# A two-layer convolution network on Trainium2: the gate's sigmoid issued at the end of the pass before its use

## The chip, the cores and the metric

The kernel runs on one NeuronCore of one Trainium2 chip. The metric is the device time of one execution in microseconds. The time before is the median of three runs.

## What is computed

The network has two layers on an input x of 8 images with 128 channels of 128 by 128, all in float32. The change touches the first layer alone. Cut to what matters, and without the batch-norm constants, that layer is:

```python
feat = gelu(bn(conv2d(x, conv_w, dilation=3)))        # 128 -> 64 channels
F2   = fft2(feat)
# attention branch: 8 heads of 8 channels
q    = F2 / l2norm(F2);  attn = complex_softmax(q @ conj(q).T * tau)
out_f = abs(ifft2(attn @ F2))
# gate branch
cg   = gelu(bn(conv1x1(F2.real)))                     # 64 -> 4 channels
cg   = sigmoid(conv1x1(cg))                           # 4 -> 64 channels
gate = abs(ifft2(cg * F2))
y    = concatenate([out_f, gate], 1) + x
```

The second layer is a 3 by 3 convolution, a Mamba scan over 8 tokens per pixel, a group norm and a silu, with a residual. It takes the first layer's result.

## The kernel before

The first layer (`layer0`) takes the images two at a time, so it has four rounds, p = 0 to 3. Each round has two parts that follow one another: `convolve(p)`, which is almost all matmul, and `spectral(p)`, in which the change lies. The order of instructions on every engine is the order in which the Python code issues them (`tc.manual_schedule` over all engines); no planner moves anything. The FFTs are matmuls against cosine and sine matrices.

`spectral(p)` is a loop of 33 passes, n = 0 to 32. Pass n works on four of the 2 x 64 channels (NP = 32 groups, the last turn only ends the last group). In the order of issue, a pass in the middle of the loop is:

- `columns(n)`: the column transforms er and ei of group n on TensorE (L293, L295), from the tile fa.
- `gate_begin(n + 2)`: four Identity activations on ScalarE (L315) that start the gate's sum cg for the group two passes ahead. They need the tile hid, which is ready early in the stage.
- `gated(n)`: four multiplies on VectorE (L335 to L338) of er and ei by the gate cg of group n, into gp.
- `rows(n + 1)`: the row transform ps of the next group on TensorE (L284) and its copy to fa on ScalarE (L286).
- `rows_back(n - 1)`: the last transform ops of the group before (L354), its Abs on ScalarE (L356), the sum with the residual on VectorE (L357, into og) and the store of og (L358) from the SP queue.
- `gate_end(n + 2)`: three multiply-add pairs on GpSimd (L325, L328; on VectorE for the first two groups), and then the sigmoid on ScalarE (L329). The sigmoid waits for the last add.
- from pass 3 on `mixture()`, which has nothing to do with the gate: it is the attention branch of four rows of the image. It has two matmuls into the tile pf (L384, L385; pf has one buffer), two squares on ScalarE (L387, L388) and a sum into feat on VectorE (L389), which frees pf. In passes 1 and 2 the softmax of the attention is done in its place, and in pass 1 this has an Exp on ScalarE (L424).
- `columns_back(n)`: eight pairs of matmuls into zps (L345, L346), and the copy to z on VectorE (L348). The next pass's ops needs z.
- in an even pass a second `mixture()`.
- `roots()`: each time that 16 rows have been mixed, a Sqrt on ScalarE over 16 rows (L399), a sum with the residual on GpSimd (L400), two stores of feat (L402), and two loads of the next residual rows (L374), all these DMAs from the SP queue.
- `load_gate(n + 3)`: a load of residual rows into xg (L365), which waits for a sum L357.

There are 32 row blocks to mix, one in an odd pass and two in an even one from pass 4 on, so they are used up in pass 24, and `roots()` does its work at the end of passes 5, 8, 10, 13, 16, 18, 21 and 24. Below these are called root passes. Passes 25 to 31 have no mixture. In an odd pass VectorE sums feat (L389) ahead of copying z (L348).

Engines execute their instructions in the order of issue, so ScalarE's queue in a pass is: L315 four times, L286, L356, L329, then L387 and L388 once or twice, and in a root pass L399. Sigmoid and Sqrt each need their own function table (ACT_TABLE_LOAD); there are 44 such loads at L329, 11 in each round.

Of the kernel before, what the change touches and what calls it, by code (L numbers as in the profile page):

```python
# [141 lines left out]
def layer0(ctx, tc, x, w0, c0, x1):  # L142
# [19 lines left out]
    def cf(name):  # L162
        at, n = C0[name]
        return ct[:, at:at + n]
# [36 lines left out]
    NP = 2 * CD // 4  # L201
# [64 lines left out]
    def spectral(p):  # L266

        with tc.tile_pool(name="l0_f1", bufs=1) as f1, \
# [11 lines left out]
            def rows(key, src, j0):  # L280

                ps = p1.tile([P, 4, P], F32, name="ps")
                for k in range(4):
                    nc.tensor.matmul(ps[:, k], src[:, :, j0 + k], cf("fwd"), start=True, stop=True)  # L284
                fas[key] = f2.tile([P, 4, P], F32, name="fa")
                nc.scalar.copy(fas[key], ps)  # L286

            def columns(key, which):

                a, out = fas.pop(key), []  # L290
                for name, of_re, of_im in (("er", "cos", "sin"), ("ei", "nsin", "cos"))[:which]:
                    e = p1.tile([P, 4, NF], F32, name=name)
                    nc.tensor.matmul(  # L293
                        e, cf(of_re), a[:, :, 0:NF], start=True, stop=False, skip_group_check=True)
                    nc.tensor.matmul(  # L295
                        e[:, :, mid], cf(of_im), a[:, :, NF:P], start=False, stop=True,
                        skip_group_check=True)
                    out.append(e)
                return out

            def hidden(b):
                er, = columns(("m", b), 1)
                for m in range(MID):
                    nc.scalar.activation(
                        hid[:, b, m, :], er[:, m, :], AF.Gelu, bias=gt[:, m:m + 1], scale=gs[:, m:m + 1])

            def place(n):
                return n * 4 // CD, n * 4 % CD

            def gate_begin(n):  # L310
                b, c = place(n)
                cgs[n] = f3.tile([P, 4, NF], F32, name="cg")
                for i in range(4):
                    k = (c + i) * MID
                    nc.scalar.activation(  # L315
                        cgs[n][:, i, :], hid[:, b, 0, :], AF.Identity, bias=b2[:, c + i:c + i + 1],
                        scale=w2[:, k:k + 1])

            def gate_end(n):

                b, c = place(n)
                eng = nc.vector if n < 2 else nc.gpsimd
                for m in range(1, MID):
                    t = f2.tile([P, 4, NF], F32, name="cgt")
                    eng.tensor_mul(  # L325
                        t, hid[:, b, m:m + 1, :].broadcast_to([P, 4, NF]),
                        w2r[:, c:c + 4, m:m + 1].broadcast_to([P, 4, NF]))
                    eng.tensor_add(cgs[n], cgs[n], t)  # L328
                nc.scalar.activation(cgs[n], cgs[n], AF.Sigmoid)  # L329

            def gated(n, e):
                er, ei = e
                cg = cgs.pop(n)
                gp = f1.tile([P, 2, 4, P], F32, name="gp")
                nc.vector.tensor_mul(gp[:, 0, :, 0:NF], er, cg)  # L335
                nc.vector.tensor_mul(gp[:, 1, :, NF:P], er[:, :, mid], cg[:, :, mid])
                nc.vector.tensor_mul(gp[:, 1, :, 0:NF], ei, cg)
                nc.vector.scalar_tensor_tensor(  # L338
                    gp[:, 0, :, NF:P], ei[:, :, mid], -1.0, cg[:, :, mid], ALU.mult, ALU.mult)
                return gp  # L340

            def columns_back(n, gp):
                zps = p1.tile([P, 4, P], F32, name="zps")
                for i in range(4):
                    nc.tensor.matmul(zps[:, i, :], gp[:, 0, i, :], cf("cos"), start=True, stop=False)  # L345
                    nc.tensor.matmul(zps[:, i, :], gp[:, 1, i, :], cf("nsin"), start=False, stop=True)  # L346
                zs[n] = f2.tile([P, 4, P], F32, name="z")
                nc.vector.tensor_copy(zs[n], zps)  # L348

            def rows_back(n):  # L350
                (b, c), z = place(n), zs.pop(n)
                ops = p1.tile([P, 4, W], F32, name="ops")
                for i in range(4):
                    nc.tensor.matmul(ops[:, i, :], z[:, i, :], cf("inv"), start=True, stop=True)  # L354
                og, xg = f2.tile([P, 4, W], F32, name="og"), xgs.pop(n)
                nc.scalar.activation(ops, ops, AF.Abs)  # L356
                nc.vector.tensor_add(og, ops, xg)  # L357
                nc.sync.dma_start(  # L358
                    x1[2 * p + b][CD + c:CD + c + 4, :, :].rearrange("c h w -> h c w"), og)

            def load_gate(n):
                if n < NP:
                    b, c = place(n)
                    xgs[n] = f3.tile([P, 4, W], F32, name="xg")
                    nc.sync.dma_start(  # L365
                        xgs[n], x[2 * p + b, CD + c:CD + c + 4, :, :].rearrange("c h w -> h c w"))
# [4 lines left out]
            def load_mixture(r0):  # L371
                mix[r0] = f2.tile([P, CH, W], F32, name="xr")
                for b in range(2):
                    nc.sync.dma_start(  # L374
                        mix[r0][b * CD:(b + 1) * CD], x[2 * p + b, 0:CD, r0:r0 + CH, :])
# [31 lines left out]
            def softmax(k):  # L407
                if k == 0:
                    nc.vector.tensor_copy(gm, gram)
                    nc.vector.tensor_mul(dg, gm, cf("ident"))  # L410
                    nc.vector.tensor_reduce(rn, dg, AX.X, ALU.add)
                    nc.vector.tensor_scalar(rn, rn, float(HW), NRM_EPS, ALU.mult, ALU.add)
                    nc.scalar.activation(rn, rn, AF.Sqrt)
                    nc.vector.reciprocal(rn, rn)
                    nc.vector.tensor_scalar(gm, gm, rn, None, ALU.mult)
                elif k == 1:
                    t = p1.tile([P, 2, 4, W], F32, name="pf")
                    nc.tensor.transpose(t[:, 0, 0, :], gm, cf("ident"))
                    nc.vector.tensor_scalar(gm, t[:, 0, 0, :], rn, tau_hw, ALU.mult, ALU.mult)
                    nc.vector.tensor_mul(gm, gm, cf("mask"))  # L420
                    nc.vector.tensor_add(gm, gm, cf("nmask"))
                    nc.vector.tensor_reduce(mx, gm, AX.X, ALU.max)
                    nc.vector.tensor_scalar(gm, gm, mx, None, ALU.subtract)
                    nc.scalar.activation(gm, gm, AF.Exp)  # L424
                elif k == 2:
                    nc.vector.tensor_reduce(rn, gm, AX.X, ALU.add)
                    nc.vector.reciprocal(rn, rn)
                    nc.vector.tensor_scalar(gm, gm, rn, None, ALU.mult)
                    t = p1.tile([P, 2, 4, W], F32, name="pf")
                    nc.tensor.transpose(t[:, 0, 0, :], gm, cf("ident"))  # L430
                    nc.vector.tensor_copy(pT, t[:, 0, 0, :])
# [7 lines left out]
            rows(0, fT, 0)  # L439
            hidden(1)  # L440
            gate_end(0)
            softmax(0)
            load_mixture(H - CH)
            load_mixture(H - 2 * CH)
            gate_begin(1)
            gate_end(1)
            for n in range(NP + 1):
                if n < NP:
                    e = columns(n, 2)
                    if n + 2 < NP:  # L450
                        gate_begin(n + 2)
                    gp = gated(n, e)
                    if n + 1 < NP:
                        b, c = place(n + 1)
                        rows(n + 1, fT, b * CD + c)
                if n > 0:
                    rows_back(n - 1)
                if n == NP:
                    break
                if n + 2 < NP:  # L460
                    gate_end(n + 2)
                if n >= START:
                    mixture()
                elif n > 0:
                    softmax(n)
                columns_back(n, gp)
                if n >= START and n % 2 == 0:
                    mixture()
                roots()
                load_gate(n + 3)  # L470
                if n == NP - 5 and 2 * p + 2 < B:
                    first_load(p + 1)
# [603 lines left out]
```

## Time and profile before

| what | value |
|---|---|
| runs, median (lowest to highest) | 15495.08 us (15492.82 to 15495.69) |
| profiled execution, its own time | 15497.77 us |
| span of the profiled execution, first to last instruction | 15495.1 us |
| mean granted TensorE clock | 0.983 |
| spectral stage of round 0, from the last Gram matmul | 333.3 us to about 662 us |
| the same of rounds 1, 2, 3 | from 988.4, 1643.7, 2299.1 us |
| second layer begins | about 2632 us |
| first ei matmul to last ei matmul of a spectral stage | 314.4, 314.7, 314.7, 314.7 us |

The profile has the start and duration of every instruction on each engine, in microseconds from the start of the span. A bracket after an instruction gives the time that its engine had been idle before it, and whose work ended that idle time. A view of waits adds such idle times up: total, number, longest. PE is TensorE's matmuls, PEld its weight loads, DVE is VectorE, ACT is ScalarE, POOL is GpSimd and SP the queue that issues DMAs. The durations of matmul groups overlap a little, since matmuls are pipelined.

A pass's length is taken here from the start of its first ei matmul to that of the next pass. In the fourth spectral stage the lengths in us are, with R for a root pass:

```
 0: 12.07   1:  6.17   2: 10.25   3:  7.82   4: 10.00   5R: 7.78   6: 18.91   7:  7.78
 8R:10.00   9:  7.78  10R:17.35  11:  7.78  12: 16.73  13R: 7.78  14: 17.94  15:  7.78
16R:10.00  17:  7.78  18R:16.87  19:  7.78  20: 17.92  21R: 7.78  22: 18.81  23:  7.78
24R: 7.78  25:  6.06  26:  8.01  27:  6.06  28:  6.06  29:  6.06  30:  6.06
```

The first three stages have the same lengths to within 0.2 us, pass by pass.

### The profile page before, as it was taken

To read this page: it belongs to the slowest core of one execution; us is meant where nothing else is said; L and a number is where in the kernel's file an instruction comes from. 1 tells how busy PE (TensorE), PEld (TensorE's weight loads), DVE (VectorE), ACT (ScalarE), POOL (GpSimd) and SP (SyncE) were. 2 spreads that over 40 slices of the span, in tenths; PEclk is the share of its full clock that TensorE was granted. 3 is DMA by queue.
4 is the path that set the end of the run, shared out by engine and by line. 5 is a ranking of instruction groups with operands and counts; after the bars stand their busy time and mean duration, and the time that the engine had idled before them with its cause. 6 is when DMAs were issued, how large, how long until landed. Compare 5 with 4: busy or idle time off the path is not lost.

```text
span 15495.1 us, 200595 instructions
## 1 busy us (share of the span) xinstructions
PE 14718.2 (95%) x71816; PEld 5738.3 (37%) x71816; DVE 12489.5 (81%) x12075; ACT 8246.5 (53%) x9158; POOL 12327.9 (80%) x6388
## 2 busy tenths in 40 slices
PE   9899898999999999999999999999999999999996
PEld 4655656333333333333333333333333333333332
DVE  1211213999999999999999999999999999999995
ACT  1322414555555555555555555555555555555553
POOL 0321304899999999999999999999999999999996
PEclk9999999999999999999999999999999999999997
DMA  1322324666666666666666666666666666666665
GB/s 73 105 74 94 82 77 103 119 117 120 120 128 135 137 136 133 135 135 134 136 135 134 135 132 135 136 137 134 135 134 135 134 137 134 136 132 135 135 136 137
DMA packets 1075749, 1932.47 MB, mean 125 GB/s; under 512 B 123969, under 2 KB 255041, under 8 KB 1058369
## 3 DMA queue, kind: packets, MB, share of 16 engines
q1 hardware_dynamic: 1074176, 1917.29, 57.7%
q8 instruction: 570, 9.34, 0.2%
q14 instruction: 427, 3.49, 0.1%
q10 hardware_dynamic: 576, 2.35, 0.0%
HBM read 375.64 MB, written 201.33 MB: 37 GB/s over the span
## 4 chain that ended last, share of the span: by engine, by line
PE 58%; DVE 17%; issue 4%; ACT 3%; DMA 1%; POOL 0%; DVEq 0%; SPq 0%; POOLq 0%; ACTq 0%
PE da L696 18%; PE yps L762 8%; PE ups L696 7%; PE pm L134 7%; DVE da L727 6%; DVE h L735 4%; DVE h L711 4%; PE yps L768 4%; PE pm L648 3%; PE pm L781 3%; PE pm L660 3%; DVE hc L746 2%; PE da L641 2%; PE yps L752 2%; ACT da L701 2%
## 5 line engine op out<-in xcount | busy, mean ns | idle before, releaser
L741 POOL TENSOR_TENSOR hc<-h,cc 128x1024 f32<-128x1024 f32 x3584 | 8377.8, 2371 | 430.5 <-DVE h L735 407.8
L701 ACT ACTIVATE da<-da 128x1024 f32<-128x1024 f32 x3584 | 3618.7, 1010 | 4193.3 <-PE ups L696 2492.3
L711 DVE TENSOR_TENSOR h<-ups,bb 128x1024 f32<-128x1024 f32 x3584 | 4368.7, 1219 | 690.3 <-issue 312.0
L696 PE MATMUL da<-du,m_a 16*128 16x512 f32 x14336 | 4061.5, 643 | 143.1 <-DVE hc L746 135.0
L696 PE MATMUL ups<-du,m_u 16*128 16x512 f32 x14336 | 4108.2, 641 | 2.5 <-DVE h L711 1.4
L735 DVE TENSOR_TENSOR h<-da,h 128x1024 f32<-128x1024 f32 x2304 | 2821.2, 1224 | 79.2
L727 DVE TENSOR_TENSOR da<-da,h 128x1024 f32<-128x1024 f32 x2304 | 2820.2, 1224 | 5.7 <-ACT da L701 2.1
L134 PE MATMUL pm<-xin,l_wt 128*128 128x508 f32 (+1 forms) x4608 | 2412.8, 624 | 177.1 <-ACT xr L786 170.2
L733 POOL TENSOR_TENSOR h<-ah,h 128x1024 f32<-128x1024 f32 x768 | 1819.0, 2368 | 442.7 <-DVE ah L725 405.0
L696 PEld LDWEIGHTS da<-du,m_a 16*128 16x128 f32 x14336 | 1077.3, 183 | 2622.3 <-issue 1001.4
L762 PE MATMUL yps<-hc,l_ct 128*32 128x512 f32 x14336 | 1927.4, 610 | 0.9 <-POOL hc L741 0.9
L134 PEld LDWEIGHTS pm<-xin,l_wt 128*128 128x128 f32 x4608 | 751.9, 189 | 1621.1 <-issue 1396.4
L325 POOL TENSOR_TENSOR cgt<-hid,l_wt 128x260 f32<-128x260 f32 x360 | 226.6, 630 | 1403.5 <-DVE cg L328 1403.5
L696 PEld LDWEIGHTS ups<-du,m_u 16*128 16x128 f32 x14336 | 1123.7, 183 | 384.5 <-DVE h L711 302.0
L241 DVE COPY fT<-tps 128x512 f32<-128x512 f32 x128 | 88.6, 692 | 1182.9 <-PE tps L240 1182.9
L701 ACT ACT_TABLE_LOAD x774 | 993.0, 1283 | 30.0 <-PE ups L696 1.0
L725 DVE TENSOR_TENSOR ah<-da,h 128x1024 f32<-128x1024 f32 x768 | 933.1, 1215 | 0.0
L134 PE MATMUL cps<-xin,l_wt 128*64 128x500 f32 (+1 forms) x4032 | 869.0, 584 | 0.0
L655 POOL TENSOR_TENSOR u<-dt,xc 128x512 f32<-128x512 f32 x512 | 656.4, 1282 | 187.4 <-ACT dt L650 187.4
L762 PEld LDWEIGHTS yps<-hc,l_ct 128*32 128x32 f32 x14336 | 283.4, 108 | 1371.7 <-issue 958.9
L235 ACT ACTIVATE feat<-cps,bn_t,bn_s 128x512 f32<-128x512 f32 x128 | 99.5, 777 | 1166.8 <-PE cps L134 1166.8
L650 ACT ACT_TABLE_LOAD x511 | 655.6, 1283 | 27.9 <-DMA cc<-bc 2.1
(156 smaller groups left out, 15310.6 us busy)
## 6 DMA issues: line engine op xcount, KB each, us to landing
bb<-bc SPq DMA_DIRECT2D x2048, 256.0 KB
cc<-bc SPq DMA_DIRECT2D x2048, 256.0 KB
du<-dt SPq DMA_DIRECT2D x2048, 64.0 KB
du<-u SPq DMA_DIRECT2D x2048, 64.0 KB
xin<-x SPq DMA_DIRECT2D x112, 640.0 KB
xin<-x SPq DMA_DIRECT2D x48, 1408.0 KB
gn<-xr SPq DMA_DIRECT2D x256, 256.0 KB
v<-gn SPq DMA_DIRECT2D x256, 256.0 KB
```

What stands on the lines that cost most here:

```text
L134: nc.tensor.matmul(out[:, a:b, wa:wb], wt[:, t, :], src[:, r + dy + a - base:r + dy + b - base, wa + dx:wb + dx], start=(n == 0), stop=(n ...
L650: nc.scalar.activation(d["dt", hf], ps, AF.Softplus, bias=wf("dt_b"))
L655: nc.gpsimd.tensor_mul(d["u", hf], d["dt", hf], d["xc"][:, hf, :])
L696: nc.tensor.matmul(o, w, v, start=True, stop=True)
L701: nc.scalar.activation(da, da, AF.Exp)
L711: nc.vector.tensor_mul(h, d["ups", s], state_row(i, "bb", s // GP))
L725: nc.vector.tensor_mul(d["ah"], da, before)
L727: nc.vector.tensor_mul(da, da, before)
L733: nc.gpsimd.tensor_add(h, d["ah"], h)
L735: nc.vector.tensor_add(h, d["da", s], h)
L741: nc.gpsimd.tensor_mul(hc, d["h", s], state_row(i, "cc", t))
L762: nc.tensor.matmul(d["yps"][g * DI:(g + 1) * DI], gather[:, t % LP, :], d["hc", GP * t + g // GP][:, g % GP], start=False, stop=(t in (3, ...
```

## The change

The sigmoid is taken out of `gate_end` and gets a function of its own, `gate_close`. For groups 2 to 31 it was issued two passes ahead of its use, in `gate_end(n + 2)` of pass n. Now `gate_close(n + 1)` is issued in pass n, behind `columns_back(n)`, which is behind the first mixture's squares and ahead of the second mixture, the Sqrt and the next pass. The multiply-add pairs on GpSimd stay where they were, two passes ahead. The sigmoid of group 0 stays in its place ahead of the loop; that of group 1 moves from ahead of the loop into pass 0. In the changed kernel ScalarE's queue has as many instructions and as many table loads (44 at the sigmoid) as before.

```diff
                     eng.tensor_add(cgs[n], cgs[n], t)
+
+            def gate_close(n):
                 nc.scalar.activation(cgs[n], cgs[n], AF.Sigmoid)
...
             gate_end(0)
+            gate_close(0)
             softmax(0)
...
                 columns_back(n, gp)
+                if n + 1 < NP:
+                    gate_close(n + 1)
                 if n >= START and n % 2 == 0:
                     mixture()
                 roots()
```

## The prediction

> **What bounds the kernel now.** I read the page's time slices first: the spectral stages are the places in the first fifth of the span where TensorE falls to 8 tenths. Then I took busy time by stretch for three of their passes, the waits of one stage, and the instructions of each engine, in order of time, around one long pass. By stretch (us; then busy time and count for PE, PEld, DVE, ACT and POOL; granted clock; DMA share; GB/s), passes 8, 9 and 10 of the fourth stage, each from its first er matmul:
>
> ```profile
> 2390.43:2398.60 8.17, 7.94 (x46) 6.59 (x44) 3.89 (x9) 3.64 (x8) 3.38 (x5) 1.00 0.28 79
> 2400.43:2408.20 7.77, 7.77 (x45) 6.61 (x44) 2.71 (x6) 7.49 (x11) 3.05 (x1) 1.00 0.01 2
> 2408.20:2425.50 17.30, 12.02 (x50) 8.86 (x49) 4.59 (x9) 5.92 (x13) 9.39 (x13) 0.80 0.77 182
> ```
>
> Pass 9 has TensorE busy throughout (the first row leaves out pass 8's second mixture). Pass 10, with 5 matmuls more, lasts 9.5 us longer, and its clock is 0.80. No engine is full in it: it is a pass of waits. The waits of this stage name them:
>
> ```profile
> DVE feat L389 <- ACT pf L388: 114.9, 32, 7.4
> ...
> ACT cg L329 <- POOL cg L328: 70.3, 26, 5.3
> ```
>
> and those of TensorE alone are
>
> ```profile
> PE pf L384 <- DVE feat L389: 21.2, 9, 6.6
> PE ops L354 <- DVE z L348: 20.9, 5, 5.0
> ```
>
> TensorE waits for VectorE, VectorE for ScalarE's squares, ScalarE for GpSimd. Pass 9 into 10, engine by engine, shows why:
>
> ```profile
> 2405.15 4.53 POOL L400 TENSOR_TENSOR feat<-feat,xr 128x2048 f32<-128x2048 f32 x1 [10.08 <-ACT feat L399]
> 2409.62 0.64 POOL L325 TENSOR_TENSOR cgt<-hid,l_wt 128x260 f32<-128x260 f32 x1
> ...
> 2413.14 0.73 POOL L328 TENSOR_TENSOR cg<-cg,cgt 128x260 f32<-128x260 f32 x1
> ```
>
> ```profile
> 2406.77 0.58 ACT L356 ACTIVATE ops<-ops 128x512 f32<-128x512 f32 x1
> 2407.37 1.28 ACT L329 ACT_TABLE_LOAD   x1
> 2413.90 0.42 ACT L329 ACTIVATE cg<-cg 128x260 f32<-128x260 f32 x1 [5.25 <-POOL cg L328]
> 2414.23 0.58 ACT L387 ACTIVATE sq<-pf 128x512 f32<-128x512 f32 x1
> 2414.84 0.58 ACT L388 ACTIVATE pf<-pf 128x512 f32<-128x512 f32 x1
> ```
>
> ```profile
> 2415.45 0.69 DVE L389 TENSOR_TENSOR feat<-pf,sq 128x512 f32<-128x512 f32 x1 [7.38 <-ACT pf L388]
> 2416.06 0.68 DVE L348 COPY z<-zps 128x512 f32<-128x512 f32 x1
> ```
>
> ```profile
> 2409.94 1.81 PE L284 MATMUL ps<-l_ct,fT 128*128 128x128 f32 x8
> 2416.80 2.07 PE L354 MATMUL ops<-l_ct,z 128*128 128x128 f32 x8 [5.04 <-DVE z L348]
> ```
>
> At the end of root pass 8 the sum L400 takes GpSimd for 4.53 us. Only then can gate_end(11) run, until 2413.87. The sigmoid of group 11 stands in ScalarE's queue for it, and pass 9's squares, whose matmuls were done at 2406.59, stand behind the sigmoid. Feat, z and ops follow late. The sigmoid itself is not wanted before pass 11.
>
> **What the Trainium skill says.** "TensorE: Matmul & The Clock Gate", section "Architectural detail", says that ScalarE and VectorE are strict FIFO; the trace agrees: the squares were ready at 2406.59 and ran at 2414.23. The same page, "What's actually happening", says that TensorE's clock halves after an idle window of about 3.4 us and needs as long a busy one to recover. The trace agrees: after the 5.04 us gap eight ops take 2.07 us, against 1.06 us in pass 9. "ScalarE: Activation LUTs", "What ACT_TABLE_LOAD costs", gives 1283 ns for the load and about 1380 ns more for a drain; the trace has the 1.28 us, and the load begins 0.02 us behind the Abs, so I take 1.28 and keep 2.66 as the upper end. "GPSIMD Engine Reference", section 3.1, has 4497 ns for an add of 2048 float32 elements; L400 takes 4.53 us here.
>
> **Part 1: the stalls that go.** By the pass lengths, an undisturbed pass takes 7.78 us with one mixture (3, 5, 7 and so on), 10.00 with two (4, 8, 16) and 6.06 with none (25, 27 to 30). Seven passes with two mixtures are longer, each the second pass after a root pass, or the first where the root pass is odd. In the fourth stage they have 18.91 + 17.35 + 16.73 + 17.94 + 16.87 + 17.92 + 18.81 = 124.53 us; less 7 x 10.00 that is 54.53. Pass 26 has 8.01 - 6.06 = 1.95: the sigmoid held up gate_begin and the copy fa, and TensorE waited 1.68 us. Sum 56.5 us a stage, of which 3 x 6.60 + 4 x 5.04 + 1.68 = 41.6 is idle TensorE and 14.9 is matmuls at the low clock. The other three stages give 56.2, 56.5 and 56.5: 225.6 us in all, the most that the change can give back.
>
> **Part 2: what is late next.** I place pass 9's instructions anew with the trace's durations. ScalarE: Abs ends at 2407.35, the squares take 1.19, to 2408.54. Table load to 2409.84; the sigmoid of group 10, whose sum GpSimd ended a root ago, to 2410.28. VectorE: feat to 2409.26, z to 2409.86, then gated(10), which now waits for the sigmoid: 2410.3 to 2411.7. TensorE, without a gap: ps(11) until 2411.6, ops(9) then, with z 1.7 us old; pf until 2414.4; zps(10) from about 2414.2, with gp 2.5 us old (1.1 if the load costs 2.66). Pass 10's first squares end at 2415.6, and the sigmoid of group 11 comes then; GpSimd has ended its sum at 2413.87 as before, 1.7 us earlier. So pass 10 takes 10.00 us.
>
> After an odd root pass, as 13: pass 14's Abs ends at 2463.54, pf at 2464.00, so the squares run to 2465.2, feat to 2465.9, and the second mixture's pf starts at 2466.0, 0.2 us after zps, as in pass 4. Load and sigmoid lie under its matmuls until 2467.0; the second squares are not due before 2467.7. Here the sigmoid, of group 15, needs a sum that was made before L400. That of group 16 is ready at 2470.05, and its sigmoid is not issued before pass 15's squares, some 5 us later.
>
> Pass 26: fa(27) is copied at about 2596.3, ahead of the sigmoid, so er(27) starts on time at 2598.2.
>
> In an undisturbed pass the sigmoid (0.42 us) leaves its place under the pf matmuls, where it cost nothing (squares start 0.03 us after pf with it ahead of them), for one behind the squares. Pass 8's would end at 2398.3 if it had only one mixture, 0.9 us before z is done and gated can use it. Cost 0. In a root pass it stands ahead of the Sqrt, but squares that it used to hold up by 0.35 us start earlier: 0. gate_begin comes up to 0.42 us later; GpSimd and ps have more slack than that.
>
> GpSimd's order and work are unchanged. On SP's queue nothing is moved; the stores of feat wait for L400 as before, and the load xg behind them is used more than 20 us later. One stage moves its bytes in 275 us instead of 332: from a DMA share of 0.40 to about 0.48. I count 0.
>
> **Part 3: what it adds.** At a stage's start gate_begin(2) comes earlier, but gated(0) waits for VectorE's own sums until 2316.40 as before, so passes 0 and 1 keep their length. In pass 1 the sigmoid of group 2 now stands behind the Exp, which waits for VectorE until 2329.53. With the Exp's 0.32, a table load and itself it ends at 2331.6, and gated(2) starts there instead of at 2330.05. gate_begin(4), fa(3) and Abs follow, og ends at 2334.7 instead of 2333.81, and the transpose L430, for which TensorE waits already, comes 0.9 us later. 4 x 0.9 = 3.6 us. Ends of this: 0, and 2.5 us a stage if the longer gap costs clock as well.
>
> **Sum.** The profiled execution has a span of 15495.1 us and a time of 15497.8. 225.6 - 3.6 = 222.0 us leave a span of 15273.1 and 15275.8 for its time; taken from the median of the runs, 15495.1, it gives 15273.
>
> **Rivals.**
> A. Half: the even root passes' stalls stay (passes 10, 12, 18, 20), because the margins there are the smallest, 1.7 us for the sum and 1.1 to 2.5 for gp. For it: the sigmoid of group n + 1 still stands ahead of the second squares. Against it: all margins are positive by the trace's own durations. It keeps (17.35 + 16.73 + 16.87 + 17.92 - 40) x 4 = 115.5 us of the loss: 15389.
> B. Slower: gated becomes the bound. It now needs a sigmoid that is issued behind squares, which wait for TensorE; a closed circle, TensorE - squares - sigmoid - gp - zps, could set every mixed pass. Its place is the wait of L335. An undisturbed pass has gp 3.3 us ahead of zps (2393.12 against 2396.42) and the sigmoid 0.9 us ahead of gated, so it decides from 4.2 us of lateness; to end slower by 0.2% it must take 222 + 31 us over 4 x 22 mixed passes, 2.9 us each. With 3.5 us each: 15273 + 308 = 15581. Against it: ScalarE is busy for 172 of 332 us.
> C. No effect: the squares were held by something else, a wait put down to GpSimd wrongly. Then 15495. Against it: the sigmoid starts 0.03 us after the sum ends, the squares at once behind it, and the new order on ScalarE does put them first.
>
> **How the numbers follow.** Full recovery 0.84, A 0.09, B 0.04, C 0.03. The bounds of the first: 8 us better (the 0.24 us waits of passes with two mixtures), and worse by 6 us at the starts, by 0.5 us for each of the 32 root passes, 16 us, and a rest of 10 for DMAs in denser passes: 15265 to 15305, widened by 5 us at the low end for the spread of runs. That holds some 0.8 alone, so the rivals stay outside. About 0.2%, 31 us, is what a measurement of this kernel can tell from no change: faster 0.93, same 0.03, slower 0.04.
>
> **What would show it.** The wait of the sigmoid for L328 falls from 70.3 us a stage to under 5, the 5.04 and 6.60 us gaps are gone, passes 6, 10, 12, 14, 18, 20 and 22 take 10.0 us and pass 26 6.1, a stage from first to last ei takes 259 us, and its clock nears 1. Pass 2 takes about 11.2 us. I am wrong if gated L335 waits for ScalarE by more than 2.5 us in mixed passes, if L354 still waits for z, or if a new wait on DMA shows up at L357 or L400.

## The result and the profile after

The changed kernel takes 15273.93 us (median of four runs, 15269.73 to 15278.72), against 15495.39 us for the kernel before (now the median of four runs, 15492.82 to 15497.16). The ratio is 0.9857, with a 95% interval of 0.984 to 0.9874: 221.5 us faster. The profiled execution has a span of 15267.9 us and a time of 15269.73 us. From L329 on, line numbers of the first layer are two higher than before: the sigmoid is L331, Abs L358, og L359, the squares L389 and L390, feat L391, z L350, the Sqrt L401 and the sum on GpSimd L402.

By stretch, passes 8, 9 and 10 of the fourth stage of the changed kernel, cut as for the kernel before (us; busy time and count of PE, PEld, DVE, ACT, POOL; granted clock; DMA share; GB/s):

```profile
2208.89:2217.06 8.17, 7.93 (x46) 6.59 (x44) 3.88 (x9) 3.94 (x9) 3.38 (x5) 1.00 0.67 166
2218.89:2226.66 7.77, 7.77 (x45) 6.62 (x44) 2.71 (x6) 7.48 (x12) 3.06 (x1) 1.00 0.01 3
2226.66:2236.67 10.01, 9.77 (x51) 7.47 (x50) 4.68 (x9) 5.97 (x12) 9.41 (x13) 1.00 0.76 179
```

Pass 10 lasts 10.01 us where it had 17.30, with the same 9.4 us of GpSimd in it and a clock of 1.00 instead of 0.80. GpSimd does as much as before, but no computing engine waits for it in this pass any more; only the stores of feat in SP's queue still do. From the waits of the same stage, all engines:

```profile
DVE gp L337 <- ACT cg L331: 3.6, 6, 1.5
...
ACT cg L331 <- POOL cg L328: 0.9, 1, 0.9
```

and all that are left of TensorE's own:

```profile
PE zps L347 <- DVE gp L340: 4.7, 1, 4.7
PE pf L432 <- DVE gm L430: 2.6, 1, 2.6
PE pf L386 <- DVE feat L391: 2.4, 10, 0.2
```

The sigmoid's wait for GpSimd has gone from 70.3 us to 0.9. The waits of ops for z are gone, those of pf for feat are ten of 0.2 us, and what stays is the start of the stage. Pass 9 into 10, ScalarE, then GpSimd, then VectorE and TensorE:

```profile
2225.22 0.58 ACT L358 ACTIVATE ops<-ops 128x512 f32<-128x512 f32 x1
2225.73 0.58 ACT L389 ACTIVATE sq<-pf 128x512 f32<-128x512 f32 x1
2226.34 0.58 ACT L390 ACTIVATE pf<-pf 128x512 f32<-128x512 f32 x1
2226.95 1.28 ACT L331 ACT_TABLE_LOAD   x1
2228.24 0.42 ACT L331 ACTIVATE cg<-cg 128x260 f32<-128x260 f32 x1
...
2233.98 0.41 ACT L331 ACTIVATE cg<-cg 128x260 f32<-128x260 f32 x1
```

```profile
2223.60 4.54 POOL L402 TENSOR_TENSOR feat<-feat,xr 128x2048 f32<-128x2048 f32 x1 [9.78 <-ACT feat L401]
...
2231.60 0.74 POOL L328 TENSOR_TENSOR cg<-cg,cgt 128x260 f32<-128x260 f32 x1
```

```profile
2228.70 0.43 DVE L337 TENSOR_TENSOR gp<-er,cg 128x260 f32<-128x260 f32 x1 [0.45 <-ACT cg L331]
```

```profile
2230.05 1.06 PE L356 MATMUL ops<-l_ct,z 128*128 128x128 f32 x8
```

The squares now follow the Abs at once. The sigmoid at 2228.24 is that of group 10, whose sum is long made; that of group 11 comes at 2233.98, and its sum ended at 2231.60 + 0.74 = 2232.34, 1.6 us earlier. The gated products do wait for the sigmoid here, 0.45 us, and it costs nothing: ops run without a gap, at full speed.

In every stage, the seven long passes take 10.00 us each and pass 26 takes 6.06; all the other passes from 3 on are as before. First to last ei matmul takes 258.4 to 258.6 us a stage, 1034.05 in all, against 1258.49: 224.4 us less.

### The profile page after: what moved, and what is told of

The parts are those of the page before. It is cut to its first block, busy times and chain, and to the rows that moved or that the text cites. A ratio compares the mean times of both kernels' runs of the same rounds, so it can differ in the third digit from the quotient of the medians.

```text
span 15267.9 us, 200535 instructions
## 1 busy us (share of the span) xinstructions
PE 14657.0 (96%) x71816; PEld 5702.9 (37%) x71816; DVE 12494.1 (82%) x12075; ACT 8246.1 (54%) x9158; POOL 12324.1 (81%) x6388
## 4 chain that ended last, share of the span: by engine, by line
PE 73%; DVE 18%; issue 4%; ACT 3%; DMA 1%; POOL 0%; SPq 0%; DVEq 0%; POOLq 0%; ACTq 0%
PE da L701 18%; PE yps L767 8%; PE ups L701 7%; PE pm L134 7%; PE cps L134 6%; DVE da L732 6%; DVE h L740 4%; DVE h L716 4%; PE yps L773 4%; PE pm L653 3%; PE pm L786 3%; PE pm L665 3%; DVE hc L751 2%; PE da L646 2%; PE yps L757 2%
```

## The experiments

Two theories stood against each other. *Queue*: the time was lost because ready squares stood in ScalarE's queue behind a sigmoid that waited for GpSimd. *Distance*: it was lost because the sigmoid was issued too early for its sum, and what helps is the pass more that lies between the sum and its sigmoid. The edits below are edits of the changed kernel, unless the kernel before is named.

### The sigmoid two passes ahead, but behind the squares

```diff
             gate_begin(1)
             gate_end(1)
+            gate_close(1)
...
-                if n + 1 < NP:
-                    gate_close(n + 1)
+                if n + 2 < NP:
+                    gate_close(n + 2)
```

> The sigmoid stays two passes ahead of its use, as before, but is issued at the pass's end, behind the first mixture's squares. Queue theory (what cost the time was that the squares stood behind a sigmoid that waits for GpSimd): most of the gain stays. After an even root pass the sigmoid waits until 2413.9 and the next pass's Identities, copy and Abs stand behind it, so the pass with two mixtures after it (10, 12, 18, 20) comes to about 12.2 us instead of 10.0; passes 6, 14 and 22 are 10.0; pass 26 stays at 8.0. That is 4 x (4 x 2.2 + 1.95) = 43 us above the changed kernel: about 15317. Distance theory (the gain is from issuing the sigmoid one pass later, when its sum is ready): the stalls stay, about 15495.

Measured: 15331.38 us, 0.9894 of the kernel before (0.9879 to 0.9909). Passes 6, 14 and 22 take 10.00 us. Of those after an even root pass, 12 and 20 take 11.1 to 12.1 us in the first and the fourth stage, 10 and 18 from 12.1 to 13.8; pass 26 takes 8.3 to 8.8. That is 14 us more than was expected: each pass 10 or 18 over 13 us has 3.41 us at half the clock in it, by the trace's record of the granted clock, and pass 2 takes 11.2 to 11.4. ScalarE in passes 9 and 10 of this kernel:

```profile
2269.34 0.58 ACT L390 ACTIVATE pf<-pf 128x512 f32<-128x512 f32 x1
2269.94 1.28 ACT L331 ACT_TABLE_LOAD   x1
2275.35 0.42 ACT L331 ACTIVATE cg<-cg 128x260 f32<-128x260 f32 x1 [4.13 <-POOL cg L328]
```

The sigmoid still waits over 4 us for GpSimd, but with the squares ahead of it, three quarters of the gain are there (161 of 221 us). So the order in the queue is the larger part, and the distance alone is refuted. It is the rest: what waits behind the sigmoid now is the next pass's Identities, fa and Abs.

### GpSimd's sum done twice, in both kernels

```diff
-                    nc.gpsimd.tensor_add(f, f, mix.pop(r0))
+                    m = mix.pop(r0)
+                    for _ in range(2):
+                        nc.gpsimd.tensor_add(f, f, m)
```

In the kernel before:

> The kernel before, with the sum of each root pass on GpSimd (4.53 us) done twice, so the attention branch's residual is added twice. Queue theory: the sigmoid, the squares behind it and TensorE wait for all of it, 8 root passes x 4.53 us x 4 stages = 145 us more: 15640, and passes 6, 10, 12, 14, 18, 20, 22 grow by 4.5 us each. A theory in which GpSimd is not in the chain: 15495.

Measured: 15648.48 us, 1.0099 (1.0084 to 1.0114), 156 us more than the kernel before in the same session (15492.27). In the fourth stage the seven passes grow by 3.5 to 5.6 us each and pass 26 by 5.5. The wait of the sigmoid in one stage:

```profile
ACT cg L329 <- POOL cg L328: 103.2, 26, 9.9
```

It was 70.3 with a longest of 5.3; 8 x 4.5 = 36 us would be the whole of the added work, and 33 show. GpSimd's work at a root pass is on the path of the kernel before, about one for one.

In the changed kernel:

> The changed kernel with the same doubled sum, so the attention branch's residual is added twice. Queue theory with the margins worked out: after an even root pass the sum for the sigmoid ends at 2418.4 on the clock of the kernel before, where the sigmoid is issued at 2415.6 and the second squares behind it are not due before 2418.4; after an odd one it has 0.8 us to spare. So the passes with mixtures keep 7.8 and 10.0 us; only passes 26 to 27 lose about 2 us a stage: 15274 + 8 = 15282 (15274 to 15300). If the change only shortened the wait: the same 145 us as in the kernel before, 15419.

Measured: 15317.29 us, 0.9885 (0.9868 to 0.9901), 43 us more than the changed kernel, not 8. The same addition costs 156 us in one kernel and 43 in the other, so the cover is real, but smaller than worked out. Pass 27 takes 10.0 us in three stages and 8.4 in one, instead of 6.06: the sigmoid ahead of it waits up to 5.5 us for GpSimd. The passes 10 and 18, for which the margin had been worked out, keep 10.00. But passes 8 and 16 take 11.0 to 14.1 us, and 12, 14, 20 and 22 up to 1.6 us more. VectorE in pass 8 of this kernel, and SP's queue ahead of it:

```profile
2251.07 0.69 DVE L359 TENSOR_TENSOR og<-ops,xg 128x512 f32<-128x512 f32 x1 [5.97 <-ACT cg L331]
```

```profile
2237.05 1.11 SPq L406 DMA_DIRECT2D x<-feat  x2
2238.21 4.12 SPq L376 DMA_DIRECT2D xr<-x  x2
2242.43 0.55 SPq L367 DMA_DIRECT2D xg<-x  x1
2243.03 0.51 SPq L360 DMA_DIRECT2D x<-og  x1
```

The sum into og waited 6 us. The view puts it down to the sigmoid, which had been done at 2250.15 and has nothing to do with og: where an engine that is named has no part in the operation, look for a DMA. The og of pass 6 was made at 2230.81, but its store was issued only at 2243.03, behind the stores of feat, which wait for GpSimd, and behind the loads xr. It took 8.0 us to land, where the two og stores ahead of it took 3.4 and 3.2, and the last signal of its landing, at 2250.99, is what ended VectorE's wait. So the theory was: the sum waits for one of two og buffers, whose store is late.

### The same with three buffers for og

```diff
-                og, xg = f2.tile([P, 4, W], F32, name="og"), xgs.pop(n)
+                og, xg = f3.tile([P, 4, W], F32, name="og"), xgs.pop(n)
```

> The changed kernel with the sum done twice (the residual of the attention branch is added twice), as in the run before, which came to 15317, and with three buffers for og instead of two. Theory: there passes 8 and 16 lost 1.4 to 4 us because og's sum waited for a buffer, whose store stood on SP's queue behind the stores of feat, which wait for GpSimd, and behind the loads after them. With a third buffer these passes, and 14, 20 and 22, take 10.0 us; pass 27 keeps its 10.0, since it waits for the sigmoid: 15274 + 4 x 3.9 = 15290. If the late transfer is the load xg and not the buffer: 15317.

Measured: 15278.67 us, 0.9863 (0.985 to 0.9877). Passes 8, 12, 14, 16, 20 and 22 are back at 10.00, and pass 27 keeps 9.8 to 10.0. It was the buffer. By the trace, all 128 sums into og start 0.03 us after their Abs again; with two buffers seven in each stage (in passes 8, 11, 13, 16, 19, 21 and 27) had started 1.5 to 5.1 us after it. That SP's queue made the store late is read from the order of its issues; no run moves the store. The time is 11 us below what was expected, and not by the passes: in the profiled execution the stretch from the last spectral pass to the end takes 12857.7 us, where it takes 12871.8 in the changed kernel and 12867.8 to 12880.5 in the other experiments. It goes with the clock: from the last spectral pass until some 470 us from the end, this execution has 51 us at half clock, the changed kernel's 89 and the others' 78 to 123, and the executions with more of it are the longer ones, with one pair out of order by 1 us. Nothing in this edit is known to cause that; the four runs of this kernel lie 14 us apart.

### The sigmoid at its use

```diff
                     e = columns(n, 2)
+                    if n > 0:
+                        gate_close(n)
...
-                if n + 1 < NP:
-                    gate_close(n + 1)
```

> The changed kernel with the sigmoid issued still later, at the start of the pass that uses it, ahead of that pass's Identities. Queue theory: no sigmoid ever waits for GpSimd; but after a root pass it stands behind the Sqrt and a table load (1.28 us), and the gated products wait: 1.8 us in passes 9, 11, 17, 19, about 1.2 in 6, 14, 22, about 2.2 in 25; 13 us a stage, 52 in all: 15326. Other passes keep 7.8 and 10.0 us. Rival B of the prediction (gated becomes the bound when the sigmoid is late): every pass grows, by 0.5 us or more, 15340 or more, and not by root passes.

Measured: 15320.98 us, 0.9887 (0.9873 to 0.9902). Passes 9, 11, 17 and 19 take 9.82 us, which is 2.0 more; 6, 14 and 22 take 0.6 more; pass 25 takes 8.03, 2.0 more; all others are unchanged. TensorE's wait of this kernel in one stage:

```profile
PE zps L347 <- DVE gp L340: 13.7, 6, 4.8
```

4.7 of it is the stage's start. So a late sigmoid is paid for through gp, as the prediction's case B had it, but only where it stands behind a Sqrt; in passes 6, 14 and 22 what TensorE then waits for, 0.57 us, is feat. The circle of that case doesn't close in other passes. One pass ahead is between two bounds: earlier, and other work waits behind it; later, and the products wait for it.

### The kernel before without GpSimd's sum

```diff
-                    nc.gpsimd.tensor_add(f, f, mix.pop(r0))
+                    mix.pop(r0)
```

> The kernel before without the root passes' sum on GpSimd, so the attention branch's residual is left out (its loads and the stores stay). If GpSimd's sum were the whole cause, the stalls would be gone: about 15270. Queue theory: the order on ScalarE still puts the squares behind the sigmoid, and the sigmoid behind gate_begin, which comes late after the Sqrt, and GpSimd's three pairs after that (3.5 us). So the passes 6, 10, 12, 14, 18, 20 and 22 come to about 12.5 us, neither 10.0 nor 17 to 19, pass 26 to 6.1: 15495 - 226 + 4 x 7 x 2.5 = 15340.

Measured: 15350.42 us, 0.991 (0.9896 to 0.9923). In the first stage, passes 6, 10, 12 and 14 take 12.54 or 12.55 us; the others, and those of the other stages, 12.5 to 14.2; those over 13 us have 3.41 us at half clock in them (see the last section). The sigmoid's longest wait in one stage of this kernel is

```profile
ACT cg L329 <- POOL cg L328: 36.4, 26, 3.2
```

Taking the long sum away gives 143 us and leaves 79 of the changed kernel's gain. It made the waits long, but the order made them stalls.

### The start of the stage

The sigmoid of group 2 ahead of the Exp, in the changed kernel:

```diff
                 elif n > 0:
+                    if n == 1:
+                        gate_close(2)
                     softmax(n)
                 columns_back(n, gp)
-                if n + 1 < NP:
+                if n + 1 < NP and n != 1:
                     gate_close(n + 1)
```

> The changed kernel with the sigmoid of group 2 issued in pass 1 ahead of the softmax's Exp instead of behind it. If it is the Exp and a table load ahead of this sigmoid that delays gated(2), pass 2 goes from 10.66 us back to 10.25, and nothing else moves: 1.6 us in all, 15272, which shows in the pass and not in the time. If not, pass 2 keeps its 10.66 us.

Measured: 15272.23 us, 0.9858 (0.9845 to 0.9872). Pass 2 takes 10.16 to 10.26 us instead of 10.66: it is the Exp and the load. The time can't tell it.

With that edit, the sums of group 1 on GpSimd:

```diff
-                eng = nc.vector if n < 2 else nc.gpsimd
+                eng = nc.vector if n < 1 else nc.gpsimd
```

> The changed kernel with two edits at the stage's start: the gate sums of group 1 on GpSimd instead of VectorE, and the sigmoid of group 2 ahead of the Exp. gated(0) then no longer stands behind VectorE's six operations for group 1 (2313.3 instead of 2316.4 on the clock of the kernel before), so zps(0) starts 3.1 us earlier and TensorE's gap of 4.7 us shrinks to 1.6, perhaps without the low clock behind it. Pass 0 goes from 12.0 us to 9 or below, pass 2 to about 10.25: 3.5 to 5 us a stage, 14 to 20 in all: 15257 (15250 to 15264). If group 1's sum on GpSimd is too late for gated(1), pass 1 takes the loss: 15270.

Measured: 15250.38 us in five runs (15248.5 to 15256.41), 0.9844 (0.9831 to 0.9858), the fastest of all, 23.6 us below the changed kernel and 21.9 below the run ahead of this one, and no run of either reaches into the other's spread. Pass 0 takes 8.5 us in three stages and 6.0 in one, and pass 1 still 6.17. TensorE's wait for gp in one stage of this kernel:

```profile
PE zps L347 <- DVE gp L340: 1.4, 1, 1.4
```

## Why the prediction was right

**What goes.** 225.6 us were to come back. In the fourth stage the seven passes went from 124.5 to 70.0 us and pass 26 from 8.01 to 6.06, as worked out; the same in the others. The reason given, ready squares behind a waiting sigmoid, is what the runs with the sigmoid behind the squares, with the sum twice and without the sum show. Reading the excess of whole passes, and not TensorE's idle time alone (41.6 us a stage), mattered: the low clock after the gaps was a quarter of it.

**What is late next.** Counted from pass 10's first er matmul, the sigmoid of group 10 was to end at +2.08 us and gated(10) at +3.5; they ended at +2.00 and +3.45. GpSimd's sum for group 11 was to end at +5.67 and the sigmoid to come at +7.4; they were at +5.68 and +7.32. The load took 1.28 us and the sigmoid began 0.01 us behind it, so the upper end of 2.66 us did not come in.

**SP's queue.** The zero was right, and its reason too short: it looked at the load xg, used long after, and not at the store of og, which stands in the same queue and gives back one of two buffers. Before, in passes 3 to 24 of every stage, that store landed at least 6.4 us before the buffer was written again, and all 128 sums into og started 0.03 us after their Abs. In the changed kernel the passes are shorter, and this room is used up: six of the 128, in passes 13, 21 and 27, start 0.15 to 0.67 us after their Abs, each 0.1 us after a store has landed. One of them, pass 13 of the fourth stage (the view names the Abs, which had ended at 2259.51):

```profile
2258.92 0.58 ACT L358 ACTIVATE ops<-ops 128x512 f32<-128x512 f32 x1 [0.31 <-PE ops L356]
2260.17 0.69 DVE L359 TENSOR_TENSOR og<-ops,xg 128x512 f32<-128x512 f32 x1 [2.26 <-ACT ops L358]
```

This is the new wait on a DMA at the sum into og that the prediction named as a sign of being wrong. It came, and no pass is longer for it; that it stayed so small was luck, since the prediction had not counted this room.

**What is added.** Pass 2 was to lose 0.9 us and in the fourth stage lost 0.41: gated(2) started 1.17 us later instead of 1.55, since the Exp came 0.4 us earlier than placed: one VectorE operation of the softmax took 0.29 us where it had taken 0.71. Why that was so stays open.

**The sum.** 222.0 us were forecast, 221.5 measured in the medians. That they agree to half a microsecond is luck: the four runs of one kernel spread over 4 us, those of the other over 9. The two profiled spans differ by 227.1 us: 224.4 in the passes, 5.0 in the three stretches between the stages, which were not forecast (below), -2.0 from the last spectral pass to the end and -0.4 at the start, each rounded. Case A (the stalls after even root passes stay) is what the sigmoid two passes ahead gave in part, and neither B nor C took place.

## What to carry to other kernels

An operation that waits should be queued behind the work that is ready, and no earlier than its result's use needs: on an engine that works in order, the price of an early wait is paid by whatever stands behind it. Follow the chain of waits down to the first engine whose own operand was late, and then ask what it held up that did not need it. When the sum is made, place each instruction of the next stretch anew with the trace's durations, buffers and DMA queues included, and state the margin of each: margins tell what the next change may still add. Shorter passes use up the room of everything whose pace they don't set, such as the landing of a store.

## What was not expected of the hardware

The clock of TensorE after a short gap is not the same each time. At the start of the next round's convolution TensorE has the same gap of 1.44 us in both kernels:

```profile
666.54 9.73 PE L134 MATMUL cps<-feat,l_wt 128*64 128x512 f32 x46 [1.44 <-issue]
```

```profile
611.14 9.33 PE L134 MATMUL cps<-feat,l_wt 128*64 128x512 f32 x52 [1.44 <-issue]
```

The first is before, 46 matmuls in 9.73 us, the second after, 52 in 9.33. The stretch from a stage's last ei to the next stage's first is 340.66 us in all three places before and 338.99 in the changed kernel, 5.0 us in sum. This does not come from the change as such: the changed kernel with the sigmoid at its use has 340.5 us in all three places again. Likewise, in the kernel without the sum, pass 14 has the same gap of 2.79 us in the first and the fourth stage, and takes 12.55 us in one and 14.24 in the other.

What goes with it in these traces is where the gap falls. A trace records the granted clock, and in all ten profiles of this case it changes only at multiples of 3.413 us, counted from the first record. These are the stretches between such points that hold the end of the 1.44 us gap, and the ones behind them, first before, then after (columns as above):

```profile
663.14:666.55 3.41, 1.19 (x11) 1.01 (x10) 1.38 (x2) 0.63 (x2) 0.00 (x0) 1.00 0.25 77
666.55:669.97 3.42, 3.42 (x18) 2.08 (x20) 0.00 (x0) 1.24 (x1) 0.00 (x0) 0.50 0.25 77
609.28:612.69 3.41, 1.97 (x21) 1.29 (x22) 0.69 (x1) 1.86 (x2) 0.00 (x0) 1.00 0.20 60
612.69:616.10 3.41, 3.41 (x22) 1.40 (x20) 0.00 (x0) 0.00 (x0) 0.00 (x0) 1.00 0.51 140
```

Before, TensorE was busy for 1.19 us of the stretch, and the next one ran at half clock; after, it was busy for 1.97 us, and none did. This gap, 1.40 to 1.45 us, is in the ten profiles 30 times. Nine of them began 1.9 to 2.3 us after such a point, and 3.41 us at half clock followed; the other 21 began between 0.15 us ahead of a point and 1.4 us behind it, and no low clock followed. The gap of 2.79 us is in the kernel without the sum twelve times, in passes 6, 14 and 22. Six lie in one stretch, but for 0.08 us at most, and their passes take 14.2 us; six are split between two stretches, and theirs take 12.55 or 12.56.

The Trainium skill, "TensorE: Matmul & The Clock Gate", section "What's actually happening", says that the window in which activity is judged is 3413 ns long and free-running, so that the moment of the change depends on where in it the first matmul lands. The traces agree, in the length and in this. It gives an idle window of about 3.4 us as what lowers the clock; here less was enough, a window with 1.19 us of matmuls in it. Which share of a window decides is not worked out here.
